# Four graph layers on one core: from two graphs per group to one, with a turn moved from TensorE to DRAM and three norms' sums taken elsewhere

## The chip, the cores and the metric

The kernel runs on one core of a Trainium2 chip. The metric is the time of one execution on the device in microseconds (us). A core has five engines that run side by side, each through its own list of instructions in order: TensorE (PE: matrix products, with weight loads shown apart as PEld), VectorE (DVE), ScalarE (ACT), GpSimd (POOL) and SyncE (SP, which here issues nearly all DMAs). Products land in PSUM, from where DVE or ACT must fetch them; everything else lies in SBUF (128 partitions) or in DRAM.

## The reference

64 graphs of 256 nodes with 256 features pass four layers. After each layer x becomes layernorm(x + layer(x)), without weights. `adj` is a symmetric 0/1 matrix with ones on its diagonal; all is float32.

- Layer 0: attention with 4 heads of 64. q, k, v are x times Wq, Wk, Wv plus biases; softmax over the neighbours; then Wo, bo and a layernorm with gamma and beta.
- Layer 1: h = layernorm(x) with gamma1, beta1; attention with 8 heads of 32 in which h is query, key and value; x = x + attention; then y = layernorm(x) with gamma2, beta2, and x + gelu(y W1 + b1) W2 + b2, with 1024 hidden units.
- Layer 2: Wh = x W; scores leaky_relu(s1[i] + s2[j]) over the neighbours, softmax, times Wh.
- Layer 3: scores leaky_relu((x * a0) x^T) over the neighbours, softmax, times x.

## The kernel before

The 64 graphs are handled in 32 groups of two (`G = 2`). A group's work is split into eleven Python generators, called threads here, and each `yield` ends a step. Their names: `a` (loads, mask, q, k, v, scores and products of layer 0, both graphs), `u0`, `u1` (rest of layer 0, one per graph), `z0`, `z1` (turning the normed x), `b` (attention of layer 1, both graphs), `w0`, `w1` (end of that attention and the norm after it), `c` (W1 and Gelu, both graphs), `o0`, `o1` (W2, layers 2 and 3, the store). A group has 163 steps.

The order of the steps is written out. `PLACES` gives each step of a group a place in units of a group's time, so that about six groups are under way at once; `FIRST` and `LAST` write out the order for the first and the last eight groups letter by letter. `usual_input` takes the steps in that order (lines 1186 to 1192), and `InOrder` (465 to 482) makes each engine keep the order in which its instructions were issued. All instructions that go through it have line 474 in the profile, so they are told apart by the names of their tiles. Tiles come from pools with a fixed number of buffers (`BUFS`); PSUM has two buffers `ps` of two banks (scores) and four `pm` of one bank (everything else). Every matrix product is float32 and appears in the trace as two records.

What the change touches:

- `flipped` (666 to 683) turns a 256x256 tile: two DMAs write it to DRAM (`put`), four read it back in pieces of 32 columns, 128 bytes each (`get`), and one DVE transpose of 32x32 blocks finishes it (`turn_blocks`). `DIRECT` names the flips of some groups that go over TensorE's transposes and an ACT copy instead. x, z, yT, n2 and n3 are turned over DRAM.
- `thread_w` (936 to 971) turns `oT` with four TensorE transposes, since `FO` is False; a path over DRAM stands beside it.
- `thread_a` (699 to 809) forms q and k for two graphs in products of 512 columns (734 to 744). The sums of the softmax come from a product with ones, `pz`; DVE takes the reciprocal of its 128x256 elements as `zs` (802) and ACT adds these up into `r_0` (803). `thread_u` spreads four rows of `zs` over all partitions by way of DRAM, `lines` and `rr` (811 to 833).
- `stats` (615 to 635) gives mean and variance by DVE's bn_stats and bn_aggr, and 1/sqrt and the offset on POOL; `scaled` (637) applies them on ACT. There are six norms per graph, five of them with such a scaling on ACT.
- `prepare` (1109 to 1174) folds weights once. beta2 times W1 is folded into b1 by products of one column (1119 to 1123).
- After the last group, a handful of DVE instructions (1195 to 1210) check that the input was such that the shortcuts hold; if not, `any_input` would compute everything again.

Of the kernel before, what the change touches and what calls it, by code (L numbers as in the profile page):

```python
# [8 lines left out]
F32 = mybir.dt.float32  # L9
BF16 = mybir.dt.bfloat16  # L10
I32 = mybir.dt.int32
# [27 lines left out]
B2 = True  # L39
FO = False  # L40
PA = True
MB = True
SM = False
DIRECT = {0: ('x', 'z', 'o'), 31: ('yT', 'n2', 'n3', 'o')}
BUFS = {'t': 5, 'q': 3, 'k': 2, 'v': 4, 'y': 4, 'z': 4, 'xb': 4, 'both': 3, 'xn': 6, 'mask': 4, 'e': 6, 'x0': 2, 'turned': 1, 'blk': 3, 'oT': 2, 'zs': 2, 'rr': 2, 'xT': 1, 'qT': 1, 'kT': 1}
PLACES = {
    "a": (0.00000, 0.17178, 0.56442, 0.61350, 0.66258, 0.66871, 0.69325, 0.75460, 0.79141, 0.90797, 0.92024,
        0.98773, 0.99386, 1.01227, 1.03068, 1.04908, 1.06749, 1.07362, 1.08589, 1.11043, 1.11656, 1.12883,
        1.15337, 1.17791, 1.20245, 1.20859, 1.23926,),
    "u0": (1.19018, 1.21472, 1.29448, 1.33742, 1.36810, 1.39877, 1.42945, 1.45399, 1.55828, 1.97546,),  # L50
    "u1": (1.32515, 1.38037, 1.40491, 1.41718, 1.44172, 1.44785, 1.49693, 1.67485, 1.90184, 2.28834,),
    "z0": (1.73620, 1.77914, 1.79755, 1.83436,),
    "z1": (1.98159, 2.09203, 2.25767, 2.39264,),
    "b": (2.12270, 2.15951, 2.22086, 2.22699, 2.35583, 2.36196, 2.43558, 2.46626, 2.47239, 2.47853, 2.48466,
        2.49080, 2.51534, 2.58896, 2.65031, 2.73006,),
    "w0": (2.50920, 2.55215, 2.60736, 2.68098, 2.72393, 2.80982, 2.89571, 3.04295,),
    "w1": (2.76074, 2.81595, 2.85890, 2.87730, 2.96319, 2.96932, 3.06135, 3.14724,),
    "c": (3.18405, 3.23313, 3.26380, 3.27607, 3.34969, 3.37423, 3.41104, 3.46012,),
    "o0": (3.61963, 3.63190, 3.68712, 3.74233, 3.80368, 3.85276, 3.95705, 4.00613, 4.10429, 4.13497, 4.24540,
        4.25153, 4.30061, 4.30675, 4.31288, 4.31902, 4.33129, 4.38650, 4.52147, 4.53374, 4.53988, 4.58282,  # L60
        4.60123, 4.63804, 4.65644, 4.70552, 4.77301, 4.78528, 4.82209, 4.82822, 4.84049, 4.86503, 5.09816,
        5.14110,),
    "o1": (3.52761, 3.54601, 3.57055, 3.57669, 3.71166, 3.71779, 3.74847, 3.76687, 3.87117, 3.88344, 3.94478,
        3.95092, 4.02454, 4.03681, 4.05521, 4.07975, 4.19632, 4.26994, 4.28221, 4.34356, 4.42331, 4.50307,
        4.59509, 4.62577, 4.64417, 4.84663, 4.88957, 4.91411, 4.92638, 4.93252, 4.93865, 5.01840, 5.16564,
        5.69939,),
}
FIRST = (
    "a0a0a0a1a0a0a0a0a0a0a0l0l0l0a0a0a0a0l0l0a0a0a0a0a0a0a0l0l0a0a0a0a0U0U0a1a0a0a2p0U0U0U0u0U0U0U0U0a1u0u0p0u0a1"
    "a1a1u0u0l0a2a1Z0a1a1Z0a1Z0Z0u0u0u0U0a3p0p0a1a2a2a2u0a1a1a1a1a1a1a1a1a1a1a1z0z0z0b0b0z0a1a1a1a2U1U1b0a1a1u1b0"  # L70
    "U1a2b0U1U1b0b0b0u1b0b0b0U1b0W0a3a4u1a2W0b0b0u1u1a2b0b0w0U1U1U1Z1Z1a2a2a2a2w0a2a2a2W0W0W0W0w0w0w0w0p0Z1a2a2Z1"
    "a2a2a2a2W0b1a2w0W0w0c0a2a2u1b1b1a2c0b1a2c0a3u1u1U2U2c0c0U1U2U2a3a3a3u1z1z1U2c0U2U2c0b1z1b1c0o0o0z1b1o0o0b1b1"
    "u1b1b1b1b1b1u2a3u2o0o0o0a4u2W1a3U2a3U2Z2Z2W1W1W1o0O0O0O0O0u2u2b1b1O0u2u2o0o0w1u2W1a3a3o0w1w1a3a3a3a3a3o0o0Z2"
    "O0w1O0O0a3a3a3w1W1o0W1W1w1w1a3a3a3w1u2z2O0z2Z2o0o0O0b2a3a3o0b2b2c1c1c1c1z2z2U3U3a3o0o0a5a3a3b2O0c1c1U3O0U3o0"
    "o0U3U3b2b2c1c1O0O0O0O0O0u3u3b2b2u3a4U2b2b2b2b2W2W2O0b2o1o0o0O0O0U3U3O0o1o1o0a4b2o1W2u3u3O0o0O0O0O0U3Z3o1W2o1"
    "W2O1O1b2b2o1Z3a4a4O1O1O1O1O1a4O0O0u3a4a4o1o1u2u3u3w2w2w2O0o1a4O0O0O0a4u3w2w2Z3Z3O1a4a4a4o1o1a4a4O0o0W2W2W2o1"
    "o1o1a4o1o0a4a4a4a4a4O1O1o0o0w2w2w2o0o0a5o0a4a4U4a4b3c2o1b3b3c2a4a4b3O1O1U4c2U4O1O1o0O1O1O1z3z3z3c2c2O0U4b3b3"
    "u4u4U4U4u4O1c2c2O1O1U3U4o1o1O1u4U4u4z3o1b3c2b3o1b3b3b3o0b3W3b3a5W3a5W3W3o2o1o1o1u4U4Z4O0o1o2o2o2O1O1u4b3u4O2"
    "O2O1O1o2b3b3O2a5a5a5o1o2o2O1O1O1O1O2o2o1O1O1a5o2Z4Z4a5u3w3w3O2W3W3O2W3O1o2Z4u4w3w3")
LAST = (  # L80
    "a6w4a7a7O3u5a6a6b5b5c4c4a6o2a6u6b5o3O3O3b5b5U6U6U6z5c4c4c4u6u6c4O3O3O3O3U6z5U6U6U6O3o3o3o3b5b5o3b5b5b5U6b5W5"
    "W5b5O3O3c4c4O3W5o4O3o4o4o4u6u6u6o3U6b5o3O3u6u6o3O3O3O3o3a7O4O4a7o4O4Z6u6b5b5O3O3Z6O3a7O4O4o4Z6O2O3O3a7W5O3o4"
    "a7a7o4w5o4z6o4w5w5w5W5a7a7O4O4O3w5O4a7a7a7a7o4o4a7a7a7o3o3o2o3W5W5W5Z6O3o4w5a7o3o3O4o4a7a7o3w5a7b6w5a7O4b6b6"
    "b6z6a7U7a7o4o4z6c5c5o4O4U7O4O3c5o3U7z6b6b6c5o4a7a7u7u7u6b6U7O4U7U7O4O4b6b6O4u7O4c5U7U7o3c5c5c5U6o4o4O4O4b6b6"
    "O4b6W6o4o4o5o5W6W6W6b6b6U7u7O5o5o4O5W6o5u7u7u7O4u7Z7o5O4O4o5o4Z7U7o4O4O5O5b6b6o5w6O5o4o4o5Z7Z7o5o5O4w6u7w6w6"
    "O4o4o4W6W6O4O4o5o5O4O5b7O4O4O5O5W6o5o5o4o5o3o4O5u7w6o5o5w6w6w6b7b7O5b7o5o5O5c6O5c6c6O5O5O5O5c6b7b7z7O4o5o5z7"
    "z7O5c6o4c6c6c6o6o6z7b7O5O5o6o6o4O4b7b7b7b7b7o6O5W7W7W7W7O5b7b7o6O6o5W7o6o6o5O6O6O6o5o5O5O5O5O5b7o4b7W7W7w7w7"
    "o6O6O6O6w7w7o5o6o5O5O5o5o5o5o5O4o6o6O5O5O5O5O5O6o5w7w7w7w7W7c7c7o6o6o6O5O6O6o6o6c7O6O6c7c7O6o6O6O6O6c7c7o6c7"
    "o7o5o6o6o7O6O6O6O6O6o6o5o7o7O7O7O7O7O6O6o7O6o7o7o6o6O6o6O7o7o7o7O7O7O6O6O6O6o7o7O7O7O6O6O7O7O7o7O5o7o7o7O7o7"
    "o7o6o6O7O7O7O7o7o6o6O7O7o7o6o6O6O7O7o6O7O7o7o7O7O7o7o7o7O6O6O7O7O7o6O7O7O7O7o7o7o7o7o7o7O7O7o6o7o7o7")  # L90
LETTERS = dict(a="a", U="u0", u="u1", Z="z0", z="z1", b="b", W="w0", w="w1", c="c", O="o0", o="o1", l="l", p="p")
# [358 lines left out]
def usual_input(ctx: ExitStack, tc: tile.TileContext, a: dict, out: bass.AP, flag: bass.AP):  # L450

    nc = tc.nc
    B = a["x"].shape[0]

# [49 lines left out]

    there = const.tile([P, B // G], F32, name="there")
    both_ways = const.tile([P, B // G], F32, name="both_ways")
    edges = const.tile([P, B // G], F32, name="edges")
    r_0 = const.tile([P, B], F32, name="r_0")
    if SM:
        POOL.memset(r_0, 0.0)  # L510
        few_out = const.tile([32, 32], F32, name="few_out")
    r_3 = const.tile([P, B, QB], F32, name="r_3")
    last = const.tile([P, B, QB], F32, name="last")

    def load_edges(g):
        adj = new(io, [P, TB, N], I32, "adj", 1)
        SP.dma_start(adj, a["adj"][g * G:(g + 1) * G].rearrange("b (q p) k -> p (b q) k", p=P))
        return adj

    def load_x(g):  # L520
        turned = None
        if FX and "x" not in DIRECT.get(g, ()):
            turned = new(io, [P, NC, T // 32, 32], F32, "turned")
            rows = a["x"][g * G:(g + 1) * G].rearrange("b n d -> (b n) d")
            parts = rows.rearrange("(t i) (c k j) -> k i c t j", i=32, c=NC, j=32)
            for k in range(P // 32):
                for c in range(NC):
                    SP.dma_start(turned[32 * k:32 * k + 32, c], parts[k, :, c])
        x0 = new(io, [P, TB, D], F32, "x0")
        SP.dma_start(x0, a["x"][g * G:(g + 1) * G].rearrange("b (q p) d -> p (b q) d", p=P))  # L530
        return x0, turned
# [28 lines left out]
    setup = new(act, [P, NF, T], F32, "hT", 1).rearrange("p f t -> p (f t)")  # L560
# [43 lines left out]
    if B2:  # L604
        b2m = const.tile([P, D], F32, name="b2m")
    else:
        b2m = const.tile([P, D], BF16, name="b2m")
        onesb = const.tile([P, P], BF16, name="onesb")
# [6 lines left out]
    def stats(src, twice=False, centre=False):  # L615
# [19 lines left out]
        return mv, rstd, nm, ve  # L635

# [62 lines left out]
    def thread_a(g, s):  # L699
        adj = load_edges(g) if g else first[0]  # L700
        yield
        adjb = new(io, [P, TB, N], BF16, "adjb", 1)
# [3 lines left out]
        pt = new(io, [P, G, QB, N], BF16, "adjT", 1)  # L706
        for t in range(TB):
            i, q = divmod(t, QB)
            SP.dma_start_transpose(pt[:, i, :, q * P:(q + 1) * P], adjb[:, t, :])
        yield  # L710
        s["x"], turned = load_x(g) if g else first[1]
        yield
        mask = s["mask"] = new(act, [P, G, QB * N], BF16, "mask")
        DVE.scalar_tensor_tensor(mask.rearrange("p g k -> p (g k)"), pt.rearrange("p g k q -> p (g k q)"), 1.0,
                                 adjb.rearrange("p t k -> p (t k)"), ALU.mult, ALU.min,
                                 accum_out=both_ways[:, g:g + 1])
        yield
        xT = new(act, [P, NC, T], F32, "xT")
        if FX and "x" not in DIRECT.get(g, ()):
            DVE.transpose(xT.rearrange("p c t -> p (c t)"), turned.rearrange("p c t j -> p (c t j)"))  # L720
        else:
            pts = []
            for c in range(NC):
                pt = new(ps_m, [P, T], F32, "pm", 4)
# [522 lines left out]
```

## Time and profile before

| | us |
|---|---|
| median of 3 runs (2437.55 to 2440.59) | 2439.83 |
| the profiled execution, its whole time | 2437.9 |
| its span, first to last instruction | 2436.0 |
| PE busy in it | 2393.9 |
| DVE busy | 2108.3 |
| ACT busy | 1588.5 |
| POOL busy | 689.8 |

The DMA engines moved 229.77 MB in 903821 packets, 707344 of them under 512 bytes. The page lists the busiest groups of instructions by tiles: `pm<-t,L_gnn_W` is the product with W1 (and other weights) of a turned tile t, `e<-ps` the exponential of the scores. In such a line the two numbers after the bar are the busy time in us, where overlapping instructions count once, and the mean duration of one in ns; after the next bar stands the engine's idle time just before these instructions and what ended it. In a row of the view in order of time the first number is the start in us, the second how long the group of like instructions took.

### The profile page before, as it was taken

The page shows a single profiled execution, that of the slowest core. Times are in us where ns is not written, and L with a number is a line of the kernel's source. Part 1 is how long each engine was busy: PE and PEld are TensorE (multiplying, and loading weights), DVE is VectorE, ACT ScalarE, POOL GpSimd, SP SyncE. Part 2 cuts the span into 40 slices and gives each one's busy share as a digit, 9 for nine tenths or more (in the row PEclk, how much of TensorE's full clock was granted, in tenths as well). Part 3 has the DMA queues.
Part 4 walks back from the last instruction along what each step waited for, and adds up shares of the span by engine and source line. Part 5 has one row for each costly group of instructions (what it writes and reads, how often), then busy time and mean ns, then how long its engine had stood idle before and what let it go on. Part 6 is the DMA issues. An engine that isn't in the chain of part 4 may idle for free.

```text
span 2436.0 us, 47812 instructions
## 1 busy us (share of the span) xinstructions
PE 2393.9 (98%) x15888; PEld 1813.0 (74%) x15888; DVE 2108.3 (87%) x6238; ACT 1588.5 (65%) x2703; POOL 689.8 (28%) x1804
## 2 busy tenths in 40 slices
PE   7899999999999999999999999999999999999997
PEld 4577777777777777777777777777777777777786
DVE  4988898889888889888889888898888898888974
ACT  3566776667766666766666766667766667666674
POOL 1122222332222332223332223322222332223332
PEclk8999999999999999999999999999999999999999
DMA  5334344453444544344544444534444444444321
GB/s 149 71 77 100 84 91 105 100 109 87 93 94 101 106 96 96 83 101 102 112 87 95 88 102 104 109 86 96 88 103 103 103 90 93 95 92 104 78 54 45
DMA packets 903821, 229.77 MB, mean 94 GB/s; under 512 B 707344, under 2 KB 903184, under 8 KB 903568
## 3 DMA queue, kind: packets, MB, share of 16 engines
q1 hardware_dynamic: 902064, 225.73, 42.6%
q8 instruction: 128, 2.10, 0.4%
q14 instruction: 125, 1.02, 0.2%
q10 hardware_dynamic: 1504, 0.92, 0.1%
HBM read 136.07 MB, written 82.05 MB: 90 GB/s over the span
## 4 chain that ended last, share of the span: by engine, by line
PE 91%; DVE 4%; ACT 2%; DMA 1%; POOL 1%; issue 1%; SPq 0%; DVEq 0%; POOLq 0%; ACTq 0%
PE pm L474 81%; PE ps L474 10%; DVE e L474 1%; DVE y L474 1%; DVE zs L474 0%; DVE st L474 0%; POOL rstd L474 0%; SPq L474 0%; ACT L474 0%; DMA blk<-rows 0%; DMA adj<-in_adj 0%; ACT e L474 0%; POOL nm L474 0%; DMA rows<-xn 0%; ACT xn L474 0%
## 5 line engine op out<-in xcount | busy, mean ns | idle before, releaser
L474 POOL TENSOR_SCALAR ve<-mv 128x2 f32<-128x2 f32 x448 | 155.5, 347 | 1652.5 <-DVE mv L474 1455.5
L474 PE MATMUL pm<-t,L_gnn_W 128*128 128x256 f32 x2048 | 461.8, 381 | 0.4 <-DVE t L474 0.3
L474 PE MATMUL pm<-L_gnn_W,hT 128*128 128x256 f32 x2048 | 453.5, 379 | 0.5 <-ACT hT L474 0.5
L474 ACT ACTIVATE e<-ps 128x1024 f32<-128x1024 f32 x384 | 377.5, 1020 | 83.3 <-PE ps L474 80.4
L474 PEld LDWEIGHTS pm<-t,L_gnn_W 128*128 128x128 f32 x2048 | 383.6, 190 | 63.4 <-ACT xn L474 10.3
L474 PEld LDWEIGHTS pm<-L_gnn_W,hT 128*128 128x128 f32 x2048 | 384.3, 190 | 51.2 <-ACT hT L474 1.1
L474 DVE SCALAR_TENSOR_TENSOR e<-e,mask 128x256 f32<-128x256 f32 x1024 | 363.7, 415 | 3.5 <-ACT e L474 3.2
L474 POOL TENSOR_TENSOR rstd<-ve,mhalf 128x2 f32<-128x2 f32 (+1 forms) x384 | 317.0, 826 | 32.1 <-POOL ve L474 0.2
L474 DVE BATCH_NORM_STATS2 st<-y 128x6 f32<-128x256 f32 x640 | 234.2, 408 | 3.5
L474 ACT ACTIVATE hT<-pm,b 128x512 f32<-128x512 f32 x256 | 169.6, 682 | 67.2 <-PE pm L474 66.5
L474 DVE STREAM_TRANSPOSE t<-blk 128x512 f32<-128x512 f32 x248 | 170.5, 695 | 19.5 <-DMA blk<-rows 19.5
L474 ACT ACT_TABLE_LOAD x133 | 170.6, 1283 | 6.9 <-issue 4.6
L474 ACT COPY v<-pm 128x259 f32<-128x259 f32 (+1 forms) x192 | 84.4, 444 | 133.4 <-PE pm L474 133.3
L474 DVE TENSOR_TENSOR e<-e,mask 128x1024 f32<-128x1024 f32 x128 | 150.7, 1221 | 22.8 <-ACT e L474 21.6
L474 ACT ACTIVATE xb<-y,nm,rstd 128x256 f32<-128x256 f32 x128 | 69.5, 591 | 148.1 <-DVE both L474 136.7
L474 PE MATMUL ps<-t 32*128 32x256 f32 x2048 | 154.9, 400 | 1.7 <-ACT e L474 1.7
L474 ACT ACTIVATE xn<-y,nm,rstd 128x256 f32<-128x256 f32 x256 | 138.4, 591 | 20.3 <-POOL xn L474 12.6
L474 PEld LDWEIGHTS ps<-t 32*128 32x128 f32 x2048 | 99.6, 184 | 53.2 <-issue 35.6
L474 DVE SCALAR_TENSOR_TENSOR y<-pm,r,xn 128x256 f32<-128x256 f32 x256 | 123.8, 484 | 12.8
L474 PE MATMUL pm<-L_gnn_WoT,oT 128*128 128x256 f32 x512 | 126.4, 392 | 5.1 <-DVE oT L474 5.0
L474 PE MATMUL pm<-v,q 128*128 128x260 f32 x512 | 130.6, 389 | 0.5 <-DVE r L474 0.5
L474 PE MATMUL ps<-qT,kT 64*128 64x256 f32 x1024 | 128.0, 389 | 2.6 <-ACT e L474 2.6
(133 smaller groups left out, 4252.2 us busy)
## 6 DMA issues: line engine op xcount, KB each, us to landing
blk<-rows SPq DMA_DIRECT2D x992, 64.0 KB
rows<-xn SPq DMA_DIRECT2D x248, 128.0 KB
x<-in_x SPq DMA_DIRECT2D x32, 512.0 KB
adj<-in_adj SPq DMA_DIRECT2D x32, 512.0 KB
rr<-lines SPq DMA_DIRECT2D x128, 128.0 KB
out<-xn SPq DMA_DIRECT2D x64, 256.0 KB
turned<-in_x SPq DMA_DIRECT2D x248, 64.0 KB
rows<-z SPq DMA_DIRECT2D x124, 128.0 KB
```

What stands on the lines that cost most here:

```text
L474: ins = call(*args, **kw)
```

## The change

Groups hold one graph: 64 groups, seven threads each (`a`, `u`, `z`, `b`, `w`, `c`, `o`), 93 steps, with new `PLACES`, and `FIRST` and `LAST` for 16 groups each. The other edits:

- `FO`: `thread_w` turns `oT` over DRAM, two DMAs out, four back and one DVE transpose, but for groups 0 and 63.
- `TR` and `PSR`: DVE turns `pz` in blocks of 32x32 straight from PSUM, so that the 256 sums lie along partitions; the reciprocal then takes 8 columns, and a second block transpose turns them back for `lines`.
- `SQ`: for three norms (z, and the two behind the values of layers 2 and 3) the DVE instruction that writes y also sums its rows, and two ACT Squares with a sum give the variance (`moments`).
- `XQ`: the four DMAs of a graph's turned x take both column halves each.
- beta2 is folded with 32 rows of equal columns and 256-column products; the result goes through DRAM to become a column. w1 is scaled by gamma2 on ACT.
- Several tiles get two buffers where they had one, now of half the size. The copies of the last variance are gone from the check at the end.

```
-FO = False
-DIRECT = {0: ('x', 'z', 'o'), 31: ('yT', 'n2', 'n3', 'o')}
+FO = True
+TR = True
+PSR = True
+SQ = True
+XQ = True
+DIRECT = {0: ('x', 'z', 'o'), 63: ('yT', 'n2', 'n3', 'o')}
...
+    def moments(src, sums, junk, twice=False):
+
+        k = 2 if twice else 1
+        sq = new(small, [P, QB], F32, "sq", 8)
+        for q in range(QB):
+            ACT.activation(junk[:, q, 0:D], src[:, q, 0:D], AF.Square, bias=sums[:, q:q + 1], scale=-float(D),
+                           accum_out=sq[:, q:q + 1])
+        share = float(D) ** -3
+        ve = new(small, [P, k, QB], F32, f"ve{k}", 8)
+        POOL.tensor_scalar(ve[:, 0], sq, share, EPS, ALU.mult, ALU.add)
...
+        rstd = new(small, [P, k, QB], F32, f"rstd{k}", 12)
+        POOL.tensor_tensor(rstd, ve, mhalf[:, 0:k * QB].rearrange("p (k t) -> p k t", k=k), ALU.pow)
+        nm = new(small, [P, QB], F32, "nm", 12)
+        POOL.tensor_tensor(nm, sums, rstd[:, k - 1], ALU.mult)
+        POOL.tensor_scalar(nm, nm, -1.0 / D, None, ALU.mult)
+        return rstd, nm, ve
...
+            pm = new(ps_m, [P, NC, N], F32, "pm", 4)
+            for f in range(NC):
+                for c in range(NC):
+                    matmul(pm[:, f, :], w[:, c, f * P:(f + 1) * P], xT[:, c, :], start=c == 0, stop=c == NC - 1)
+            yield
+            for f in range(NC):
+                ACT.activation(dst[:, f, :], pm[:, f, :], AF.Identity, bias=bcol[:, f:f + 1])
...
+        if PSR:
+            DVE.transpose(zs, pz)
...
+            few = new(small, [P, N // 32], F32, "few", 4)
+            DVE.reciprocal(few, turned[:, 0:N:32])
+            back = new(small, [P, 32], F32, "back", 4)
+            DVE.transpose(back, few.unsqueeze(1).to_broadcast([P, 4, N // 32]))
+            ACT.activation(few_out, few, AF.Copy, accum_out=r_0[:, g:g + 1])
+            yield
+            lines = new(dram, [NC, 2, 32, 32], F32, "lines", 4)
+            SP.dma_start(lines.rearrange("c h b i -> (c h b) i"), back)
...
+            for k in range(2):
+                f = 2 * f2 + k
+                ACT.activation(hT[:, f, :], pm[:, k, :], AF.Gelu, bias=b1[:, f:f + 1])
...
-            DVE.scalar_tensor_tensor(y[:, q, :], po[:, 0:D], r, x[:, q, 0:D], ALU.mult, ALU.add)
+            DVE.scalar_tensor_tensor(y[:, q, :], po[:, 0:D], r, x[:, q, 0:D], ALU.mult, ALU.add,
+                                     **(dict(accum_out=sums[:, q:q + 1]) if SQ else {}))
...
+        b2r = setup2[:, 1024:1088].rearrange("p (c q) -> p c q", c=NC)
+        DVE.tensor_copy(b2r, beta2.unsqueeze(2).to_broadcast([P, NC, 32]))
+        pm = new(ps_m, [P, N], F32, "pm", 4)
+        for h in range(4):
             for c in range(NC):
+                matmul(pm[32 * h:32 * h + 32, :], b2r[:, c, :], w1[:, c, h * N:(h + 1) * N], start=c == 0, stop=c == NC - 1)
+        more = setup2[:, 1280:1536]
+        ACT.copy(more, pm)
```

## Prediction

> **What bounds the kernel now.** First the page's line of busy times and its 40 slices.
>
> ```profile
> PE 2393.9 (98%) x15888; PEld 1813.0 (74%) x15888; DVE 2108.3 (87%) x6238; ACT 1588.5 (65%) x2703; POOL 689.8 (28%) x1804
> ...
> PE   7899999999999999999999999999999999999997
> ...
> PEclk8999999999999999999999999999999999999999
> ```
>
> TensorE is busy for 2393.9 of 2436.0 us, and the two slices that are not full are the first two and the last. The chain of waits says the same (91% of it is PE). The table of busy time by stage then says where the 42.1 us without PE work lie, and how full the other engines are in the middle.
>
> ```profile
> 0.00:20.00 20.00, 10.22 (x23) 5.32 (x24) 2.37 (x3) 6.69 (x10) 0.95 (x10) 1.00 0.54 160
> 20.00:40.00 20.00, 15.40 (x134) 9.09 (x132) 10.86 (x12) 10.11 (x17) 0.00 (x0) 0.99 0.48 142
> 40.00:60.00 20.00, 18.57 (x61) 14.64 (x62) 13.34 (x31) 4.06 (x7) 6.65 (x9) 0.59 0.57 141
> 60.00:100.00 40.00, 35.00 (x298) 21.45 (x296) 37.15 (x113) 25.41 (x41) 3.85 (x7) 0.96 0.29 70
> 100.00:150.00 50.00, 45.41 (x325) 33.04 (x325) 41.49 (x118) 29.44 (x45) 13.21 (x26) 1.00 0.37 80
> ...
> 600.00:1200.00 600.00, 600.00 (x4014) 454.25 (x4013) 533.67 (x1573) 399.39 (x684) 176.10 (x458) 1.00 0.45 97
> ...
> 2400.00:2420.00 20.00, 16.48 (x78) 12.87 (x76) 13.15 (x42) 9.49 (x24) 4.46 (x14) 0.91 0.00 1
> 2420.00:2436.00 16.00, 4.53 (x20) 3.65 (x20) 6.95 (x27) 5.26 (x12) 5.04 (x21) 0.78 0.21 70
> ```
>
> After the stretch come PE, PEld, DVE, ACT and POOL busy, then clock, DMA share and GB/s. 25.4 us of PE idleness lie ahead of 150 us and 15.0 us behind 2400 us; in the middle PE never rests, with DVE at 89%, ACT at 67% and the DMA engines at 45%. So the time is (PE work of a graph) x 64 plus two ends. PE's own row of time gives the first factor, and the prices that this change needs.
>
> ```profile
> 1026.43 0.66 PE L474 MATMUL pm<-ident,oT 128*128 128x128 f32 x4
> 1026.92 7.07 PE L474 MATMUL pm<-L_gnn_W,hT 128*128 128x256 f32 x32
> ...
> 1045.48 3.65 PE L474 MATMUL pm<-xT,L_gnn_WqT 128*128 128x512 f32 x8
> 1048.97 0.60 PE L474 MATMUL pm<-ident,oT 128*128 128x128 f32 x4
> 1049.41 1.90 PE L474 MATMUL pm<-xn,q 128*128 128x257 f32 x8
> ...
> 1100.26 0.66 PE L474 MATMUL pm<-ident,oT 128*128 128x128 f32 x4
> ...
> 1206.06 3.62 PE L474 MATMUL pm<-L_gnn_WvT,xT 128*128 128x256 f32 x16
> 1209.51 1.04 PE L474 MATMUL pm<-v,q 128*128 128x260 f32 x4
> ```
>
> Ends are modelled and run into the next row, so prices are taken from start to start. The same transposes come at 1026.43 and 1100.26 us: one group, two graphs, takes **73.83 us**, a graph 36.92. 32 such groups are 2362.6 us, and 2436.0 - 2362.6 = **73.4 us** is what both ends cost together.
>
> **The change on TensorE, part by part.**
> The transposes of oT (`FO`) leave PE. Four of them take 1026.92 - 1026.43 = 0.49 us at one place and 1049.41 - 1048.97 = 0.44 at the other: 0.93 us per pair, 0.465 per graph. (The group's own mean of 281 ns would say 1.1 us per graph; that is a latency.) The period becomes (73.83 - 0.93) / 2 = **36.45 us per graph**; graphs 0 and 63 keep theirs (+0.9, counted with the ends).
> One graph per group turns each 512-column product of Q and K into two of 256. Eight records of 512 columns take 1048.97 - 1045.48 = 3.49 us, sixteen of 256 (V's) 1209.51 - 1206.06 = 3.45: no cost. c and W2 were already issued in 256 columns.
> The Trainium skill speaks against it ("TensorE: Matmul & The Clock Gate", "Why this matters for your kernels": keep every dimension at 512 or more, overhead dominates below). Its 2.5 ns per start (same page, "Back-to-back issue gap") would add some 1.3 us for 512 more records, an estimate; the two rows above differ by nothing that can be seen.
> 64 x 36.45 = **2332.8 us**, 29.8 us less.
>
> **The ends.** `prepare` folds beta2 with 32 one-column records, which take 6.7 us from start to start at 45 us, at a clock of 0.59. Sixteen 32-row records of 256 columns take their place; 32 such (e,v) take 1.75 us, so 0.9: -5.8. The SP round trip that it adds is needed only by the first c, some hundred us on: hidden. The hand-named direct flips fall from 40 transposes to 20: 20 x 0.12 = -2.4. The first load is half as long: x landed at 6.2 us, and PE's first product began at 11.7, behind ACT's passes over two graphs (3.0 us from 8.7). Half of both would be -4; both have fixed parts, so -3. At the tail each of the last two norms has a Square pair on ACT (1.4 us) for 1.05 us of bn_stats and bn_aggr: +0.7; the two `last` copies (0.2 each) go: -0.4. Together 73.4 + 0.9 - 5.8 - 2.4 - 3 + 0.3 = **63.4 us**. The new written order of the ends can give or take more: not below 73.4 less three quarters of the 42 us idle (42), not above 85, which is 12 us of new waits, half of the idle time ahead of 150 us now.
>
> **The cover.** The gain is there only if nothing else comes late, so every other queue is counted per graph against 36.45 us.
>
> ```profile
> L474 DVE BATCH_NORM_STATS2 st<-y 128x6 f32<-128x256 f32 x640 | 234.2, 408 | 3.5
> L474 DVE STREAM_TRANSPOSE t<-blk 128x512 f32<-128x512 f32 x248 | 170.5, 695 | 19.5 <-DMA blk<-rows 19.5
> L474 DVE RECIPROCAL zs<-pm 128x256 f32<-128x256 f32 x64 | 112.2, 1753 | 15.7 <-PE pm L474 15.6
> L474 ACT ACTIVATE t<-t,a 128x256 f32<-128x256 f32 x128 | 58.3, 510 | 81.9 <-DVE t L474 81.9
> ```
>
> *DVE*, 32.8 us now. Out: the reciprocal of 128x256, 1.75; six bn_stats at 234.2 / 640 = 0.37, 2.2; six bn_aggr at 0.15, 0.9. In: six accumulator reads at 0.081, 0.49; one more turn, 0.69; the transpose of pz from PSUM, 0.42 on the line through 695 ns at 512 columns and 1240 at 1024 (no row has it from PSUM: between 0.3 and the reciprocal's 1.75); the small reciprocal and back-turn, 0.2 each (row r<-r: 0.234); mask, x+beta0 and xT in halves, 0.27. 32.8 - 4.85 + 2.27 = 30.2, 83%.
> *ACT*, 24.6 us now. In: six Squares with a sum. No row has them; 0.388 (zs) to 0.591 (xn) for 256 columns plus 0.188 for the read, and 0.51 (t<-t,a, one column operand) is nearest: 0.70 x 6 = 4.2 (3.5 to 4.7). Gelu in halves: 470 ns (oT<-pm,gamma) twice for 682, +1.03; qT and kT likewise +0.51; adj and adjb +0.2; the sum of `few` for that of zs, -0.2. Table loads: walking the written order and counting each change between steps with Exp and steps with Gelu gives 133, which is the page's x133; the new order gives 127, so two per graph as now. 24.6 + 5.7 = 30.3, 83%.
> *POOL* has the same five instructions for a norm, 10.7 us. *SP* issues six more DMAs per graph at 0.48 us (blk's median 487 ns), and x and adj twice as often: its 22 us (the rows of one period) become 26. The *DMA engines* get a fifth flip beside four: 45% becomes about 52%.
> The Trainium skill speaks against this flip too ("VectorE: DVE Perf Modes", "Rules for kernel authors": turn 128x128 on TensorE where PSUM will do). That would keep PE's 0.465 us and spare DVE's 0.69; by it this part loses 0.22 us per graph, 14 us, which holds only if the two engines shared one bound.
>
> What is late next: I compare gaps in the written order, counted in PE work between the step that makes a thing and the PE step that uses it. The turned x stands 5.8 us ahead of Q (0.3 before); ea, 1.9 ahead of its products (0 before); the read of rr, 22 us ahead of its use (4 to 5); w's new flip has 5.4 us from read to turn. Between each pair of Squares and the scaling that waits for POOL (1.7 us by its rows) stand at least 3.3 us of other ACT work. So I cost stalls in the middle at nothing new.
>
> **Sum.** 2332.8 + 63.4 = 2396.2 us of span; the profiled execution took 2437.9 for a span of 2436.0, so + 1.9: **2398 us**, that is 1.7% below the median of 2439.83 (the profiled execution lies 1.9 us below it).
>
> **Rivals.**
> *ACT's queue becomes the wait (slower).* It goes from 67% to 83%, in order, and the exponentials that free PE's two ps buffers stand in the same queue as the Squares. For it: ACT already waits for PE at e<-ps 80 us in all, so it runs close behind. Against: 6 us free per graph. It decides from (2439.8 - 2398) / 64 = 0.65 us of PE wait per graph; one Square pair (1.4 us) late before one exp per graph gives 2398 + 90 = 2488 us.
> *The turn over DRAM is late (part of the gain lost).* 12 of 248 turns came late now, 19.5 us of DVE waits; a fifth flip and a fuller SP queue could make it 0.45 us of PE per graph: 2398 + 29 = 2427.
> *The middle is better than counted.* At the cheapest rate of each kind PE's 73.83 us are about 72.6, so up to 0.6 us per graph are bubbles between rows. Looser gaps could close half, 19 us, and better ends 10 more: 2369.
>
> **Chances.** The forecast, 2376 to 2416: 0.60. Late DRAM turn, 2416 to 2445: 0.12, a third of it within 0.2% of the median, which is about what a measurement tells from no change. ACT's queue: 0.16. Better than counted: 0.12. So faster 0.80, same 0.04, slower 0.16. The range takes in the bounds of the ends (-21, +22) and most of the second and fourth case: 2362 to 2430.
>
> **What would show it.** The period in PE's row near 36.45 us; no pm<-ident,oT in the middle; 127 table loads; ACT and DVE each near 83%; PE idle only ahead of 150 us and in the last 36. Wrong would be: PE waits of over 0.6 us per graph with ACT e or DVE t as the releaser, a Square that costs more than 0.8 us, or a transpose from PSUM near 1.75.

## The result, and the profile after

The changed kernel takes **2408.94 us** (median of 4 runs, 2405.76 to 2411.14) beside 2438.97 for the kernel before (4 runs, 2437.55 to 2440.59): a ratio of 0.9876, 95% interval 0.9859 to 0.9893. The forecast was 2398, so 11 us of the 41 it promised are missing. The profiled execution took 2405.76 us for a span of 2404.0.

The page of the changed kernel, busy times, slices and the chain of waits:

```profile
PE 2351.7 (98%) x16116; PEld 1873.4 (78%) x16116; DVE 1924.6 (80%) x6175; ACT 1827.0 (76%) x3975; POOL 739.3 (31%) x1740
...
PE   7899999999999999999999999999999999999997
...
PEclk9999999999999999999999999999999999999999
...
PE 41%; DVE 24%; DMA 13%; SPq 8%; ACT 6%; POOL 5%; issue 3%; DVEq 0%; ACTq 0%; POOLq 0%
```

PE lost 42.2 us of work and the span only 32.0. The slices look as they did. The chain does not: PE held 91% of it, now 41%; DVE, DMA and SP's queue stand on it as well. Somewhere in the middle PE now waits for a path that ends outside it. The table of busy time by stage of the changed kernel (columns as in the prediction) shows where:

```profile
0.00:20.00 20.00, 10.85 (x42) 8.62 (x44) 1.30 (x3) 7.27 (x16) 0.93 (x10) 1.00 0.65 159
20.00:40.00 20.00, 16.76 (x112) 12.25 (x109) 12.54 (x22) 11.74 (x26) 0.00 (x0) 1.00 0.54 137
40.00:60.00 20.00, 20.00 (x191) 14.34 (x193) 18.22 (x42) 14.15 (x34) 5.44 (x7) 1.00 0.69 150
...
600.00:1200.00 600.00, 593.07 (x4094) 472.25 (x4083) 487.33 (x1574) 462.11 (x1010) 192.66 (x440) 1.00 0.52 112
1200.00:1800.00 600.00, 599.03 (x4123) 480.81 (x4122) 492.57 (x1582) 472.71 (x1026) 197.76 (x448) 1.00 0.53 113
```

Before, 600:1200 held 600.00 us of PE; now it is 593.07. Over the whole stretch from 150 to 2250 us PE stands idle for 16.1 us, where it had 0.7. PE's row in order of time says what a wait costs (the bracket holds the idle time before the row and what ended it):

```profile
1264.48 0.33 PE L474 MATMUL pm<-ident,q 128*128 128x128 f32 x1
1300.68 0.33 PE L474 MATMUL pm<-ident,q 128*128 128x128 f32 x1
1335.23 1.93 PE L474 MATMUL pm<-e,v 128*32 128x256 f32 x32 [0.81 <-ACT oT L474]
1338.60 0.33 PE L474 MATMUL pm<-ident,q 128*128 128x128 f32 x1
```

The row pm<-ident,q comes once per graph. Undisturbed, a graph takes 1300.68 - 1264.48 = **36.20 us**, less than the 36.45 forecast. The next one takes 37.92, 1.72 us more. Most of it, 1.34 us, comes where a product waits until ACT has copied oT out of PSUM (from the start of the products (e,z), at 1332.14, to that of (e,v) pass 3.09 us instead of 1.75), of which the trace shows only 0.81 as idle; another 0.31 lies in the scores of layer 0 before them.

The costs of single instructions came out as forecast. Groups of the changed kernel, shapes kept apart (after the bar busy us and mean ns, then the idle time before them):

```profile
L474 DVE STREAM_TRANSPOSE t<-blk 128x512 f32<-128x512 f32 x314 | 214.0, 693 | 295.5 <-DMA blk<-rows 295.5
L474 ACT ACT_TABLE_LOAD x127 | 162.9, 1283 | 8.4 <-DMA L_gnn_WkT<-in_L_gnn_WkT 6.8
...
L474 ACT ACTIVATE xn<-y,sums 128x256 f32<-128x256 f32 x256 | 127.5, 499 | 59.3 <-DVE y L474 58.6
...
L474 DVE STREAM_TRANSPOSE zs<-pm 128x256 f32<-128x256 f32 x64 | 27.0, 421 | 1.3 <-PE pm L474 1.3
```

A Square takes 0.499 us, with its read of the accumulator (0.188) 0.69, where 0.70 was taken; the transpose from PSUM 0.421 (0.42 taken); 127 table loads. What stands out is the first line's end: DVE waits 295.5 us for blocks read back from DRAM, where it was 19.5.

**Where the wait comes from.** SP's row and, below it, DVE's around 650 us of the changed kernel:

```profile
645.88 0.49 SPq L474 DMA_DIRECT2D lines<-back  x1
648.01 1.28 SPq L474 DMA_DIRECT2D rr<-lines  x2
649.33 2.18 SPq L474 DMA_DIRECT2D blk<-rows  x4
```

```profile
654.55 0.71 DVE L474 STREAM_TRANSPOSE t<-blk 128x512 f32<-128x512 f32 x1 [4.42 <-DMA blk<-rows]
```

SP writes `lines` to DRAM and has its read back, `rr`, next in its list. The read is made to wait until the write has landed, so SP stands until 648.01, 2.13 us after the write's start. Behind it in the same list waits the block read of n3 in thread `o`. That read starts at 649.33, the blocks land, and DVE, which has that turn next in its own list, has stood for 4.42 us. All DVE work behind it is late, the turn of z among it, and ACT, which keeps its order too, passes that on: at another such place, where DVE has stood for 5.31 us (until 1023.85), ACT then stands 1.69 us (until 1038.68) for DVE's t, the turned z, and its copy of oT behind that comes 0.80 us late for PE (at 1041.17). In `PLACES` the write stands at 3.21505 and the read at 3.22581 of a period: 0.39 us apart. The Trainium skill bears on it ("DMA: Bandwidth & Descriptors", "Anatomy of one DMA — SWDGE (gpsimd) path"): a DMA engine doesn't wait for semaphores; the issuing sequencer does, ahead of the dispatch. The rows agree for SP's queue: the read of `rr` is issued 2.13 us after the write, and the block read only behind it.

Not every such stand reaches PE. DVE's turn of n3 in two graphs that follow each other:

```profile
1279.60 0.71 DVE L474 STREAM_TRANSPOSE t<-blk 128x512 f32<-128x512 f32 x1 [3.87 <-DMA blk<-rows]
1317.91 0.71 DVE L474 STREAM_TRANSPOSE t<-blk 128x512 f32<-128x512 f32 x1 [5.22 <-DMA blk<-rows]
```

The first lies in a period of 36.20 us, the second in the one of 37.92. The 28 periods up to 1338.60 us are together 16.7 us longer than 28 x 36.20; there DVE mostly stands for 4.2 to 5.3 us. The 19 periods that follow are all 36.19 or 36.20, though SP and DVE stand there too, DVE for 3.8 to 4.3 us. Why the wait is shorter there was not looked into.

### The profile page after: what moved, and what is told of

It is laid out like the page before. It is cut to its first block, busy times and chain, and to the rows that moved or that the text cites. A ratio compares the mean times of both kernels' runs of the same rounds, so it can differ in the third digit from the quotient of the medians.

```text
span 2404.0 us, 49948 instructions
## 1 busy us (share of the span) xinstructions
PE 2351.7 (98%) x16116; PEld 1873.4 (78%) x16116; DVE 1924.6 (80%) x6175; ACT 1827.0 (76%) x3975; POOL 739.3 (31%) x1740
## 3 DMA queue, kind: packets, MB, share of 16 engines
q8 instruction: 130, 2.13, 0.4%
## 4 chain that ended last, share of the span: by engine, by line
PE 41%; DVE 24%; DMA 13%; SPq 8%; ACT 6%; POOL 5%; issue 3%; DVEq 0%; ACTq 0%; POOLq 0%
PE pm L474 36%; SPq L474 8%; DMA blk<-rows 7%; DVE e L474 6%; DVE y L474 4%; PE ps L474 4%; DVE t L474 3%; DMA lines<-back 3%; POOL nm L474 2%; ACT e L474 2%; DVE st L474 2%; POOL rstd L474 2%; DVE q L474 2%; ACT xb L474 1%; DMA turned<-in_x 1%
## 5 line engine op out<-in xcount | busy, mean ns | idle before, releaser
L474 PE MATMUL pm<-L_gnn_W,hT 128*128 128x256 f32 (+1 forms) x2064 | 462.5, 379 | 0.0
L474 DVE STREAM_TRANSPOSE t<-blk 128x512 f32<-128x512 f32 x314 | 214.0, 693 | 295.5 <-DMA blk<-rows 295.5
L474 PEld LDWEIGHTS pm<-L_gnn_W,hT 128*128 128x128 f32 (+1 forms) x2064 | 384.9, 189 | 51.5 <-issue 0.7
L474 POOL TENSOR_SCALAR ve<-mv 128x2 f32<-128x2 f32 x192 | 70.3, 366 | 1061.7 <-DVE mv L474 1033.7
L474 ACT ACTIVATE hT<-pm,b 128x256 f32<-128x256 f32 x512 | 206.3, 470 | 21.2 <-PE pm L474 18.7
L474 POOL TENSOR_SCALAR ve<-sq 128x2 f32<-128x2 f32 x256 | 67.1, 262 | 496.3 <-ACT xn L474 407.5
L474 ACT ACTIVATE xn<-y,sums 128x256 f32<-128x256 f32 x256 | 127.5, 499 | 59.3 <-DVE y L474 58.6
L474 ACT ACTIVATE xn<-y,nm,rstd 128x256 f32<-128x256 f32 x256 | 139.3, 595 | 12.2 <-POOL nm L474 7.4
L474 POOL TENSOR_SCALAR nm<-nm 128x2 f32<-128x2 f32 x320 | 132.0, 413 | 28.0
L474 PE MATMUL pm<-e,v 128*32 128x256 f32 x2048 | 123.4, 381 | 12.1 <-ACT oT L474 9.7
L474 PE MATMUL pm<-xT,L_gnn_WqT 128*128 128x256 f32 x512 | 125.0, 388 | 7.0 <-ACT xT L474 4.5
```

The lines of the kernel that those rows point to most:

```text
L474: ins = call(*args, **kw)
```

## The experiments

**Is it this order of SP's list? `e3_rr_later`** moves one step of the changed kernel, the read of `rr`, behind the read of n3's blocks:

```
-    "u": (3.06452, 3.21505, 3.22581, 3.68817, ...
+    "u": (3.06452, 3.21505, 3.35000, 3.68817, ...
```

> The changed kernel with one step of every middle graph moved: the read of rr (third step of u, place 3.226) goes to 3.350, just behind the read that feeds the n3 turn, so that SP no longer waits for the write of lines to land ahead of that read. Theory: this wait in SP's queue is what makes the n3 turn late on DVE; DVE's waits for blk fall from 295 us to under 200, PE idleness in the middle from 16 us to under 8: 2396 to 2404 us. Rival: the turn is late because of the landing time or the place of its own read, or DVE's waits do not reach PE: 2406 to 2412 us.

Measured: **2384.46 us** (2382.74 to 2386.92), ratio to the kernel before 0.9781 [0.9768, 0.9795]. SP's row and the stages of e3_rr_later:

```profile
602.30 0.49 SPq L474 DMA_DIRECT2D lines<-back  x1
602.89 1.97 SPq L474 DMA_DIRECT2D blk<-rows  x4
604.96 1.28 SPq L474 DMA_DIRECT2D rr<-lines  x2
```

```profile
600.00:1200.00 600.00, 600.00 (x4129) 483.05 (x4129) 497.83 (x1590) 474.98 (x1029) 180.32 (x446) 1.00 0.54 114
1200.00:1800.00 600.00, 600.00 (x4183) 481.73 (x4180) 501.52 (x1594) 474.35 (x1029) 181.15 (x447) 1.00 0.53 115
```

The block read now starts 0.59 us after the write, inside the time in which SP used to stand. DVE's waits for blocks fall from 295.5 to 104.5 us, PE is busy for all of 600 us in both stages, and the kernel gains 24 us: more than was expected. The period is 36.20 in every row read (1210.84, 1247.04, 1283.23).

**Or is it DVE's order? `e7_turn_later`** leaves SP as it was and moves DVE's turn of n3 back, so that other DVE work stands ahead of it:

```
     "o": ( ... 9.18280, 9.34409,
-        9.36559, 9.62366,
+        9.47850, 9.62366,
```

> The changed kernel with one step of every middle graph moved: DVE's n3 turn (21st step of o) from place 9.366 to 9.4785, some 4 us later; SP's order is untouched. Theory: DVE standing still in front of this turn, with other work behind it, is how SP's wait reaches PE; so this cures as much as moving the read of rr did: 2382 to 2395 us, DVE's waits for blk under 200 us. Rival: other reads behind SP's wait come late too, and only the move in SP's queue helps: 2402 to 2411 us.

Measured: 2386.28 us (2384.35 to 2387.8), 0.9782 [0.9768, 0.9795]; DVE waits for blocks 84.9 us; PE again 600.00 of 600.00 us in both stages. Two cures that touch different engines' lists give the same time. In e7 SP stands for `lines` as long as in the changed kernel (85.1 us in all, there 87.0; 12.6 in e3), so that only DVE's order has changed. The cause is shown: SP standing for a landing *and* DVE standing first for the read behind it. With either taken away, the middle has no stall left.

**The turn of oT back on TensorE: `e1_turn_on_pe`**, and **`e10_clean_turn_on_pe`** with the cure of e3 as well:

```
-DIRECT = {0: ('x', 'z', 'o'), 63: (...)}
+DIRECT = {**{g: ('o',) for g in range(64)}, 0: ('x', 'z', 'o'), 63: (...)}
```

> The changed kernel with one part undone: oT of every graph goes over TensorE's transposes and PSUM again, in the same written order (the step that read the DRAM copy is empty). Theory: PE's work sets the time, so 62 graphs get their 0.465 us back, +29 us on 2409, less up to 10 us because DVE and SP have one turn less and so the 16 us of PE idleness in the middle shrink: 2428 to 2438 us, period about 36.85 us. Rival: the gain came from the other parts (grouping, ends, less DVE work) and the turn over DRAM gives back in waits what it saves on PE: 2405 to 2413 us.

> The changed kernel with rr's read moved and oT turned on TensorE in all groups. Theory: with no waits in the middle the turn's price on PE stands alone, 62 x 0.465 = 29 us on 2384.5: 2410 to 2416 us, period 36.20 + 0.465 = 36.67 us; so 22 to 28 us of the distance to the kernel before come from the other parts. Rival: waits for PSUM buffers come with the transposes and stay: 2420 us or more.

Measured: 2441.86 (1.0013 [1.0004, 1.0022]) and 2441.58 (1.0015 [1.0006, 1.0024]). Both lie above what was expected of the turn's price alone; e10 came out as its rival had it, 2420 or more by a wait for PSUM buffers. The cure that was worth 24 us is worth nothing here. PE's row of e10_clean_turn_on_pe, and one line of DVE's below it, tell why:

```profile
1203.68 0.33 PE L474 MATMUL pm<-ident,q 128*128 128x128 f32 x1
...
1204.71 0.60 PE L474 MATMUL pm<-ident,oT 128*128 128x128 f32 x4
1205.15 1.89 PE L474 MATMUL pm<-t,L_gnn_W 128*128 128x256 f32 x8
...
1210.06 1.99 PE L474 MATMUL pm<-xT,L_gnn_WqT 128*128 128x256 f32 x8 [0.43 <-ACT hT L474]
...
1241.01 0.33 PE L474 MATMUL pm<-ident,q 128*128 128x128 f32 x1
```

```profile
1211.38 0.69 DVE L474 TENSOR_TENSOR y<-pm,r 128x512 f32<-128x512 f32 x1
```

The transposes take 1205.15 - 1204.71 = 0.44 us. But the period is 1241.01 - 1203.68 = 37.33, which is 1.13 above 36.20; the other 0.69 us is a wait that comes 48 times in PE's list of waits, once per graph of the middle. Q's product reads xT and Wq and nothing of Gelu's, so what Gelu (hT) sets free can only be the PSUM buffer that it reads: the turned oT lies in PSUM from 1204.71 until DVE fetches it at 1211.38, and that is one tile too many for the four `pm`. That last step is argued from the program and these rows; it was not tried with another buffer. The turn on TensorE costs 57 us against e3: 62 x 0.44 = 27 of work and 48 x 0.69 = 33 of this wait come to 60, and the difference of 3 was not taken apart.

**bn_stats for all norms: `e2_bn_stats`**, and **`e11_clean_bn_stats`** with the cure:

```
-SQ = True
+SQ = False
```

> The changed kernel with SQ undone: the three norms take mean and variance from bn_stats and bn_aggr on DVE again, and ACT loses its six Squares per graph. Theory: the 16 us of PE idleness in the middle come from DVE running late behind turns that wait for DRAM, not from ACT; with some 2.6 us per graph more on DVE they grow: 2412 to 2440 us, DVE busy near 2090 us. Rival: the Squares in ACT's queue cause them; they vanish with the Squares: 2390 to 2400 us.

> The changed kernel with rr's read moved and SQ undone: bn_stats and bn_aggr on DVE for all norms. Theory one: DVE at 84% has room, and it was the late n3 turn on top that made undoing SQ cost 67 us; with that turn in time it costs little: 2385 to 2400 us. Theory two: DVE's 2.6 us per graph move its steps behind their places in an order written for less, whatever the turn does: 2430 to 2460 us.

Measured: 2476.07 (1.0158 [1.0144, 1.0172]) and 2479.44 (1.0175 [1.0162, 1.0189]). The sign of the theories that gave DVE a part was right, the size larger than they had. A row of PE in e11_clean_bn_stats and, below it, one of ACT from the same period:

```profile
1228.80 3.72 PE L474 MATMUL pm<-L_gnn_W,hT 128*128 128x256 f32 x16 [1.95 <-ACT hT L474]
```

```profile
1226.94 1.09 ACT L474 ACTIVATE xn<-y,nm,rstd 128x256 f32<-128x256 f32 x2 [3.69 <-POOL nm L474]
```

In each graph of the middle W2's product waits for Gelu (48 times, 63.6 us in all, at most 2.1), and the periods are 37.5 to 38.5 us. It is not the DRAM turn: DVE's waits for blocks are 42.5 us in e11, fewer than in e3. DVE is at 86 and 85% in the two middle stages, in e3 at 83 and 84%, so it isn't a full engine either. The trace says which step comes late: the scaling of a norm (xn), which stands ahead of that Gelu in ACT's list. It needs POOL's nm, POOL needs DVE's mv, and DVE's bn_stats of this y start only at 1224.24, behind a turn and two operations on another y. So the scaling starts at 1226.94 and the Gelu at 1227.94; at the same place of e3's period (its start 1210.84, here 1212.67) they start at 1222.28 and 1223.26. ACT waits 151.9 us for POOL's nm before xn in e11, 7.9 in e3.

**The reciprocal of all 128x256 elements: `e4_long_reciprocal`** undoes `TR` and `PSR` in the changed kernel (with one empty step, so that the order stays):

```
-TR = True
-PSR = True
+TR = False
+PSR = False
...
         else:
+            yield
             lines = new(dram, [NC, 2, N], F32, "lines", 4)
```

> The changed kernel with TR and PSR undone: DVE takes the reciprocal of all 128x256 elements of pz, ACT adds them up, and four rows go to DRAM; the first step of u is empty. Theory: DVE gets some 0.95 us per graph more; with 6 us free per graph most of it is hidden, and what is not shows as more PE idleness in the middle: 2409 to 2422 us. Rival one: PE hides it all, 2406 to 2411 us. Rival two: DVE is near its limit because of the waits in its queue, and nearly all of it reaches the time: 2440 to 2470 us.

Measured: 2429.63 us (2426.82 to 2430.07), 0.996 [0.9946, 0.9973]: 20.7 us above the changed kernel, somewhat more than expected. DVE's busy time rises by 67.8 us (1.06 per graph), so about a third of that arrives at PE, and PE's list shows new waits for Gelu (20.1 us) and for ACT's sum of `zs`, which writes over the PSUM tile (8.6).

**The old fold of beta2: `e8_old_fold`**, and **`e9_clean_old_fold`** with the cure: 32 one-column records and an ACT copy again, in place of 16 records and the way over DRAM.

```
+        pm = new(ps_m, [P, NF], F32, "pm", 4)
+        for f in range(NF):
             for c in range(NC):
-                matmul(pm[32 * h:32 * h + 32, :], b2r[:, c, :], ...
+                matmul(pm[:, f:f + 1], w1[:, c, f * P:(f + 1) * P], beta2[:, c:c + 1], ...
```

> The changed kernel with the fold of beta2 undone: 32 records of one column on PE, one ACT copy in place of the two DMAs, one step left empty. Theory: these products stand in PE's way while it is the bound or cools its clock down, +5.8 us: 2412 to 2417 us. Rival: PE has idle time nearby that takes them up: 2406 to 2411 us.

> The changed kernel with rr's read moved (2384.5 us, no PE wait in the middle) and the fold of beta2 undone as before. With the middle free of waits the fold is seen alone. Theory: the one-column products cost PE some 5.8 us while it is the bound: 2388 to 2392 us; the 15 us of the earlier run were mostly waits in the middle that the later start brought on. Rival: the fold itself costs those 15 us, by way of the clock or of what follows it: 2397 to 2402 us.

Measured: 2423.95 (0.9928 [0.9915, 0.9942]) and 2385.57 (0.9786 [0.9773, 0.9799]). With the cure the old fold costs 1.1 us between the medians, less than either expectation. In e9 its records take 4.94 us from start to start and the new ones 1.01 in e3; but in e3 PE then waits 2.00 us for DVE's oT, which the longer fold covers. By 78 us e9 is 3.7 us behind, and after that it runs as e3 does. Without the cure the same edit costs 15 us, more than either expectation of e8 had: PE idles for 29 us between 150 and 2250 us, not 16. The stalls, which come in only some groups of the changed kernel, then go on for longer.

**Parts alone, in the kernel before.** `e5_before_flip` sends oT over DRAM in the old order, write and read in one step; `e6_before_flip_sums` adds the sums from the writing pass and the Squares; `e12_before_flip_spaced` is e5 with write and read in steps of their own (the scaling and the write of yT share one instead).

```
-FO = False
+FO = True
...
-            yield
             blk = get(rows)
...
-            if FO:
-                yield
             yield
```

The diff is that of e5; e12 keeps the first of these steps, and has this instead:

```
         scaled(xb, x2, mv, rstd[:, 0], nm)
-        yield
         yield from flip_to(g, s, "yT", i, xb, not FY)
```

> The kernel before with one part of the change alone: oT is turned over DRAM (FO) in 30 of its 32 groups, write and read in one step so that its written order fits. PE's work alone would give 60 x 0.465 = 28 us: 2408 to 2414 us. Theory: the turn pays only where DVE has room; here DVE goes from 89% to 93% of the period and w1's turn stands close behind its read, so most of the gain goes into waits: 2425 to 2450 us, with waits of DVE for blk well above the 19.5 us of before.

> The run before this one with a second part: the three norms' sums come from the writing pass and from ACT's Squares (SQ), still two graphs per group in the old written order. Theory: DVE's relief (some 2.6 us per graph) is what lets the turn over DRAM pay: 2408 to 2425 us, below the kernel with the turn alone by 15 us or more. Rival: the Squares, in an order that was not written for them, hold up ACT and what waits for it: 2430 us or more.

> The kernel before with the turn of oT over DRAM alone, as in the run that took 2838 us, but with write and read one place apart (the scaling and the write of yT share a step instead). Theory: there SP stood in front of the write until oT was ready and then until the write had landed, and everything behind it came late; apart, the second wait goes and most of the loss with it: 2480 to 2650 us, still above the kernel before, since w1's turn then stands 1 us behind its read. Rival: the place of the turn on DVE is what costs, not SP: 2750 us or more.

Measured: 2837.67 (1.163 [1.1614, 1.1646]), 2995.52 (1.2279 [1.2262, 1.2296]) and 2719.9 (1.1162 [1.1146, 1.1177]). The expectation of 2425 to 2450 for e5 missed by 390 us: the part that the forecast counts as the gain makes the old kernel 16% slower. The theory that DVE's relief makes the turn pay fell with e6. e12 takes away the landing wait between write and read and wins back 118 us of 399; its time lies between its theory's (2480 to 2650) and its rival's (2750 or more). What SP's own list waits for in e12_before_flip_spaced (total us, times, longest):

```profile
SPq L474 <- ACT oT L474: 303.5, 42, 12.2
```

The old order gave the write of oT no time: SP stands up to 12.2 us for the tile, with every other load and flip behind it. That this stand is what costs the remaining 281 us was not tried. Why e6 is worse than e5 was not settled; PE there waits most for DVE's `r` (206.8 us in all), in e5 for ACT's `v` (147.4).

## Why the prediction was right, and where it was wrong

- **What bounds the kernel: right.** The time is PE's work per graph times 64 and two ends. Without stalls in the middle (e3) the span is 2382.7 us, 64 x 36.20 and 65.9 for both ends. (Three slices of the page before are not full, the first two and the last, where the prediction counts two; nothing rests on it.)
- **The turn off TensorE, 0.465 us per graph: right.** Measured in place: 0.44 (e10). That the products of 256 columns cost nothing is right too: eight records for Q take 1216.19 to 1217.92 in e3, 1.73 us per graph, 3.46 per two, where eight of 512 took 3.49.
- **The period, 36.45: a little too long.** It is 36.20, 16 us over 64 graphs. Compared row by row from start to start, per two graphs, the products (e,z) fell from 3.73 to 3.50, those for 8 heads' scores from 4.53 to 4.32, those of wx from 3.71 to 3.52, and those with W1 from 14.01 to 13.80. Other rows rose, V's products most (3.46 to 3.65), so that 0.50 is left, 0.25 per graph. Those are bubbles between rows, which the third rival had named; 0.25 of its 0.6 us per graph came.
- **The ends, 63.4: nearly right, by errors that cancel.** e3 has 65.9. The fold was put at -5.8 and is worth 1.1 to 3.7: its old price had been read at a granted clock of 0.59, and its cover was not looked at. The first product starts 1.5 us earlier (10.23, was 11.72), not 3.
- **The cover: right, for the engines.** In e3's middle DVE is at 83% (83 forecast), ACT at 79% (83), the DMA engines at 53% (52). ACT's queue never became the wait: PE's waits for ACT's exponentials come to 2.3 us in the whole changed kernel, and the slower rival did not come.
- **"So I cost stalls in the middle at nothing new": this step failed.** It is worth 2404.0 - 2382.7 = 21.3 us, 16.7 of it in the 28 periods named above. The step compared, for each thing, when it is made and when it is used; by that measure the read of `rr` had become *safer* (22 us ahead of its use, 4 to 5 before). It did not ask what SP must wait for to *start* that read, 0.39 us behind the write, and what stands behind it. This is the second rival, the late DRAM turn, with a price of 29 us (21 measured) and the right wait (DVE's t for blk); but it was put down to a fuller queue, not to one wait inside it.
- **The sum.** 2398 - 16 (period) + 2.5 (ends) + 21.3 (stalls) = 2405.8, which is the profiled execution's time. It closes by construction, as three of its terms are measured in these two traces. That the forecast lies only 11 us off is in part luck: the period was missed by 16 us the other way, and with the measured period the same sum would have been 27 us too low.
- **The weighed rule** (the Trainium skill, "VectorE: DVE Perf Modes", "Rules for kernel authors": turn 128x128 on TensorE). The runs speak both ways: in the new order following it costs 57 us (e10 against e3), in the old order leaving it costs 281 to 399 (e12, e5 against before).

Not shown: what grouping by one graph and the new ends bring by themselves. They cannot be had without a new written order. With the turn back on TensorE the rest gains nothing (1.0015), but 48 x 0.69 = 33 us of that is the PSUM wait, which another order might avoid.

The best version is the changed kernel with one step moved (e3): 2384.46 us, 1.0% below the changed kernel and 2.2% below the one before.

## What to carry to other kernels

In a queue that issues in order, a read that waits for an earlier write's landing blocks everything behind it: put the next independent transfers between the two, here by moving one step an eighth of a period, for 24 us. When a written order is judged by gaps, count for each instruction what it waits for at its own start and who is queued behind it, not only how far ahead of its use it stands. A part that frees the bounding engine (oT's turn) is worth what the order around it allows: the same edit was worth 57 us in one order and cost 16% in another.

## What the runs showed of the hardware that was not expected

- **A stall can hide in a busy engine.** The changed kernel and e3 issue the same 16116 matmul records, but PE counts 2351.7 us busy in the one and 2340.9 in the other; a period with a stall is 1.72 us longer and shows 0.81 idle. Periods from start to start say what a wait costs, idle time does not.
- **A lower granted clock goes with long waits of TensorE, not with their sum alone.** The mean over the span is 0.996 in the changed kernel, 0.957 in e12, 0.939 in e5 and 0.926 in e6, in the order of PE's idle time (52, 246, 329 and 438 us). But e2 has 116 us of it, twice that of the changed kernel, at 0.998; its many waits for Gelu last at most 1.9 us each, the main ones of e12, e5 and e6 up to 5.3, 7.3 and 8.7. Whether the length of one wait decides was not tried. A row can carry the clock of its place: the 32 one-column records took 6.68 us in the kernel before, at 0.59 in their stage, and 4.94 in e9, at 0.91.
